# Edge-by-edge graph layers on one core: one tile of every second block by products, 0/1 matrices compared from a broadcast row, x kept in DRAM

## Chip, core and metric

One Trainium2 chip, one core. The metric is the device time of one execution in microseconds (us). A trace of one profiled execution stands beside it.

## The reference

Two graph layers over 6250 nodes with 128 features and 200000 edges, which come sorted by their destination:

```python
h = relu(layernorm(x))
z = h @ W                                  # 8 heads of 16
el, er = per-head dot products of z with attn_l, attn_r
e = leaky_relu(el[src] + er[dst], 0.2)
a = exp(e - segment_max(e, dst)[dst])
agg = segment_sum(z[src] * a, dst); out = agg / segment_sum(a, dst)
x = x + out + bias
h = relu(layernorm(x))                     # second layer
s, v = 32 scalars and 32 vectors of h, each multiplied by a weight
w0..w3 = two-step silu network of edge_attr_8, 128 weights per edge
mji = products of s[src], v[src], edge_attr_4 and w0..w3
x = x + linear(segment_sum(mji, dst) / 10)
```

Rows of a node table are thus taken by src (in any order) for each edge, and sums go to dst.

## The kernel before

The edges lie in tiles of 128, one edge to a partition; 16 tiles (KB) make a block, and there are 98 blocks (NB). Since the edges are sorted, the destinations of one block fall into a window of 128 nodes, of which 64 (WB) begin each next block. A table in DRAM holds one row of 136 floats for each node in the first layer (t0: z and el) and one of 128 in the second (t1). `gather` fetches 128 rows of a tile with one indirect DMA that POOL issues (L832), 16 for a block, into a buffer `g` (pool `fz`, five of them).

In every third block (`by_row`, from block 3) the last of the 16 tiles is fetched otherwise: SP reads 32 offsets into registers (L1063) and issues one DMA of 544 bytes for each of the 128 rows (L1067); ACT copies the finished tile `r` into `g` (`filled`, L1081). The generator `rows_by_row` spreads these issues: `rows_until` moves it on in each block, and its rows stand three blocks ahead of the block that uses them. There are three `r` buffers.

In the first layer the loop runs over blocks g. PE, DVE, ACT and SP keep the order of the program (`manual_schedule`); POOL's gathers for block g + 3 begin as a buffer comes free. In an iteration three blocks are in work: the logits and running maxima of g (`logits` L1163, `maxima`), the softmax weights, weighting and sums of g - 1 (`neighbours`, `weights`, `weighted`, `sums` L1221), and for g + 1 the destination's er. That last needs the 0/1 matrix of a tile the other way round: DVE compares the edges-by-nodes matrix `s` (`ends_of`, `one_hot` L1086, for g + 2), PE turns each by a transpose into `p_d` (`turned`, L1138), ACT casts four of them to bf16 `d` (L1140), and PE multiplies them with the three bf16 parts of er (`er_of`, L1149). Every odd block completes 128 nodes, which in the iteration after next run through `node_x`, `node_d`, `node_h`, `node_t`, `node_s` to become rows of t1; SP stores them (`node_out`, L1281) in the iteration after that. x stays in SBUF as `fx_all` through both layers.

The second layer has a loop of its own over the same blocks, with the same gathers and rows from t1.

Of the kernel before, what the change touches and what calls it, by code (L numbers as in the profile page):

```python
# [741 lines left out]
def tile_even_edges(  # L742
# [87 lines left out]
    def gather(to, table, tiles, width):  # L830
        for k, t in enumerate(tiles):
            nc.gpsimd.indirect_dma_start(  # L832
                out=to[:, k, :width], out_offset=None, in_=table,
                in_offset=bass.IndirectOffsetOnAxis(ap=src_col[:, t : t + 1], axis=0))
        return to
# [128 lines left out]
def even_edges(tc, v):  # L964
# [7 lines left out]
    with ExitStack() as ctx:  # L972
        const = ctx.enter_context(tc.tile_pool(name="fconst", bufs=1))
        z_pool = ctx.enter_context(tc.tile_pool(name="fz", bufs=5))

        def gathered(table, tiles, width):
# [7 lines left out]
        nc.sync.dma_start(rsel, v["rsel"])  # L984
        x_all = const.tile([P, NX, P], F32, name="fx_all")
        bias_b = const.tile([P, F], F32, name="fbias_b")
# [6 lines left out]
        nc.sync.dma_start(a2p, v["a2p"])  # L993
        a3p = const.tile([P, 2, P], F32, name="fa3p")
        nc.sync.dma_start(a3p, v["a3p"])
        b1 = const.tile([P, 1], F32, name="fb1")
        nc.sync.dma_start(b1, v["b1"])
        b2 = const.tile([P, 1], F32, name="fb2")
        nc.sync.dma_start(b2, v["b2"])
        wout = const.tile([P, 2, P], F32, name="fwout")  # L1000
        nc.sync.dma_start(wout, v["wout"])
        dloc = const.tile([P, NB * KB], F32, name="fdloc")
# [10 lines left out]
        with tc.tile_pool(name="fbuild", bufs=1) as build:  # L1013
# [9 lines left out]
            nc.sync.dma_start(off, nums[:, :TU])  # L1023
            nc.vector.tensor_sub(dloc[:, :TU], d_c, off)


# [17 lines left out]
        at = [const.tile([P, P], I32, name=f"fat{i}") for i in range(2)]  # L1044
        with tc.tile_pool(name="fat_ps", bufs=1, space=PSUM) as at_ps:
            col = const.tile([P, P], F32, name="fcol")
            n = NB - 1
            nc.vector.tensor_copy(col[:, :n], v["src_col"][:, KB - 1 : n * KB : KB])
            p_c = at_ps.tile([P, P], F32, name="p_c")
            nc.tensor.transpose(p_c[:n], col[:, :n], ident)  # L1050
            for i, w in enumerate((ZW, P)):
                nc.vector.tensor_scalar(at[i][:n], p_c[:n], float(4 * w), None, op0=OP.mult)
# [38 lines left out]
        def finish(b, p_u, width, carry, agg, pool):  # L1091
# [6 lines left out]
            else:  # L1098
# [4 lines left out]


        in_order = {mybir.EngineType.PE, mybir.EngineType.DVE, mybir.EngineType.Activation,
                    mybir.EngineType.SP}
        with tc.manual_schedule(engines=in_order), \
                tc.tile_pool(name="l0", bufs=2) as l0, \
                tc.tile_pool(name="l0n", bufs=2) as l0n, \
                tc.tile_pool(name="l0_ps", bufs=1, space=PSUM) as l0_ps:  # L1110

            p_n = l0_ps.tile([P, 512], F32, name="p_n")
            er_p, iota_p = p_n[:, P : 2 * P].rearrange("p (t h) -> p t h", h=H), p_n[:, 3 * P :]
            nc.scalar.copy(iota_p, iota)


# [5 lines left out]
            def masks_of(c):  # L1124
# [6 lines left out]
                nc.scalar.copy(mk[:kr], p_m[:kr, :MC])  # L1131

            def turned(c, q):
                if 4 * q < c["kt"]:
                    m = min(4, c["kt"] - 4 * q)
                    p_d = l0_ps.tile([P, 4, P], F32, name="p_d", bufs=2)
                    for k in range(m):
                        nc.tensor.transpose(p_d[:, k, :], c["s"][q][:, k, :], ident)  # L1138
                    d = c["d", q] = l0.tile([P, 4, P], BF, name="d", bufs=4)
                    nc.scalar.copy(d[:, :m], p_d[:, :m])  # L1140

# [16 lines left out]
            def logits(c, bank="pe"):  # L1158
                kt = c["kt"]
                kr = kt * H  # L1160
                e_s = l0.tile([P, KB, H], F32, name="e_s")
                pe = c["pe"] = p_n if bank == "p_n" else l0_ps.tile([P, 512], F32, name=bank, bufs=2)
                nc.vector.tensor_add(e_s[:, :kt], c["z"][:, :kt, F:], c["er"][:, :kt])  # L1163
# [59 lines left out]


            def node_rows(i, n):
                nc.sync.dma_start(x_all[:, i : i + n, :],
                                  xp[i * P : (i + n) * P].rearrange("(j p) f -> p j f", p=P))

            def with_bias(i, n):
                x_i = x_all[:, i : i + n, :]  # L1230
                nc.vector.tensor_add(x_i, x_i, bias_b[:, None, :].to_broadcast([P, n, F]))

            def node_x(u):
                i, n, agg = u["i"], u["n"], u["agg"]
                x_i = x_all[:, i : i + n, :]
                if n == 1:
# [13 lines left out]
            def node_h(u):  # L1250
                i, n = u["i"], u["n"]
                rs, mr = normal(l0n, u["mv"], u["rs"], n, f"n{n}")
                xn = u["xn"] = l0n.tile([P, 2, P], F32, name="xn")
                nc.scalar.activation(xn[:, 0, :], x_all[:, i, :], AF.Identity, bias=mr[:, 0, :],
                                     scale=rs[:, 0, :])
                if n == 2:
                    nc.vector.tensor_scalar(xn[:, 1, :], x_all[:, i + 1, :], u["mv"][:, 1, 0:1],
                                            rs[:, 1, :], op0=OP.subtract, op1=OP.mult)

            def node_t(u):  # L1260
                n = u["n"]
                u["p_n"] = p_n.rearrange("p (j f) -> p j f", f=P)
                for j in range(n):
                    nc.tensor.transpose(u["p_n"][:, j, :], u["xn"][:, j, :], ident)
                h_t = u["h_t"] = l0n.tile([P, 2, P], F32, name="h_t")
                nc.scalar.activation(h_t[:, :n], u["p_n"][:, :n], AF.Relu)

# [7 lines left out]
            def node_out(u):  # L1275
                i, n, sv = u["i"], u["n"], u["sv"]
                first = i * P - W0
                if i == 0:
                    nc.sync.dma_start(t1[: P - W0, :], sv[W0:, 0, :])
                else:  # L1280
                    nc.sync.dma_start(t1[first : first + n * P].rearrange("(j p) f -> p j f", p=P),  # L1281
                                      sv[:, :n])

            groups = [(b, 0, KB) for b in range(NB - 1)]
# [11 lines left out]
            def take_rows(g):  # L1296
                if 0 < g < NG:
                    c = cs[g]
                    t = c["b"] * KB + c["o"]
                    c["z"] = gathered(t0, range(t, t + c["kt"] - (c["b"] in by_row)), ZW)  # L1300

# [27 lines left out]
            for g in range(1, 3):  # L1329
                take_rows(g)  # L1330
            masks_of(cs[0])
            for q in range(4):
# [13 lines left out]
            for g in range(NG - 3):  # L1346
# [11 lines left out]
                nodes = []  # L1358
                logits(c)
                ends_of(n2, 0)  # L1360
                if n1 is not none:
                    masks_of(n1)
                turned(n1, 0)
                maxima(c)
                ends_of(n2, 1)
                if b4:
# [3 lines left out]
                turned(n1, 1)  # L1370
                er_of(n1, 0)
                if b4:
                    weights(b4)
                for n in nodes:
                    node_x(n)
                er_of(n1, 1)
                turned(n1, 2)
                if b4:
                    bank_of(b4)
                    weighted(b4, 0)  # L1380
                turned(n1, 3)
                er_of(n1, 2)
                if b4:
                    weighted(b4, 8)
                for n in nodes:
                    node_d(n)
# [3 lines left out]
                if b4:  # L1390
                    sums(b4, 0)
                for n in nodes:
                    node_t(n)
# [6 lines left out]
                if b4:  # L1400
                    sums(b4, 8)
                if g == NG - 4:
                    for q in range(4):
# [63 lines left out]
        with tc.manual_schedule(engines=in_order), \  # L1467
                tc.tile_pool(name="l1", bufs=3) as l1, \
                tc.tile_pool(name="l1n", bufs=2) as l1n, \
                tc.tile_pool(name="l1_ps", bufs=2, space=PSUM) as l1_ps:  # L1470

            def edge_rows(b):
# [71 lines left out]
            def sums1(u):  # L1544
# [3 lines left out]
                for k in range(m):  # L1548
                    nc.tensor.matmul(blk[b]["p_u"][:, :MW], u["s"][:, k, :], u["mj"][:, k, :],  # L1549
                                     start=k0 + k == 0, stop=k0 + k == KT[b] - 1)  # L1550

            def node1(i, agg):
                x_i = x_all[:, i, :]
                p_n = l1_ps.tile([P, 4, P], F32, name="p_n", bufs=1)
# [9 lines left out]
            def node_out1(i):  # L1564
                x_i = x_all[:, i, :]
                if i == 0:
                    nc.sync.dma_start(out[: P - W0, :], x_all[W0:, 0, :])
                else:
# [16 lines left out]

            rows, rows_until.n, late = rows_by_row(1, t1, P), 0, []
            for b in range(2):
# [9 lines left out]
            for i, u in enumerate(us):  # L1597
                b, k0, m = u["b"], u["k0"], u["m"]
                if k0 == 0:
                    take_rows(b + 2)  # L1600
                    filled(1, b, blk[b]["z"], P)
                    edge_rows(b + 2)
                if k0 == 4:
                    while late:
# [36 lines left out]
            for j in range(2):  # L1641
                for q in range(2):
                    nc.tensor.matmul(p_o[:, j, :], m_t[:, 2 * j + q, :], wout[:, q, :],
                                     start=q == 0, stop=q == 1)
            x_i = x_all[:, NX - 2 :, :]
            nc.vector.scalar_tensor_tensor(x_i, p_o[:, :2], POST, x_i, op0=OP.mult, op1=OP.add)
# [139 lines left out]
```

## Time and profile before

| | us |
|---|---|
| median of three runs (6300.1 to 6317.29) | 6316.72 |
| the profiled execution | 6201.12 |
| its span | 6199.2 |
| busy: PE / weight loads / DVE / ACT / POOL | 2970.3 / 2462.3 / 2207.9 / 1390.7 / 2919.2 |
| first layer: first and last start of L1163 in the trace | 178.6 to 2976.8 |

An engine's busy time is summed over the span; a group's line gives line, engine, operation, operands, count, then its busy time and mean ns, then the idle time just before its instructions and what ended most of it. DMA issues are not counted as busy. In the timeline a line gives the start, the length, the engine and the number of merged instructions.

### The profile page before, as it was taken

To read this page: it belongs to the slowest core of one execution; us is meant where nothing else is said; L and a number is where in the kernel's file an instruction comes from. 1 tells how busy PE (TensorE), PEld (TensorE's weight loads), DVE (VectorE), ACT (ScalarE), POOL (GpSimd) and SP (SyncE) were. 2 spreads that over 40 slices of the span, in tenths; PEclk is the share of its full clock that TensorE was granted. 3 is DMA by queue.
4 is the path that set the end of the run, shared out by engine and by line. 5 is a ranking of instruction groups with operands and counts; after the bars stand their busy time and mean duration, and the time that the engine had idled before them with its cause. 6 is when DMAs were issued, how large, how long until landed. Compare 5 with 4: busy or idle time off the path is not lost. (4 is left out here: it accounts for less than half of the span.)

```text
span 6199.2 us, 62249 instructions
## 1 busy us (share of the span) xinstructions
PE 2970.3 (48%) x14593; PEld 2462.3 (40%) x14593; DVE 2207.9 (36%) x5379; ACT 1390.7 (22%) x3612; POOL 2919.2 (47%) x3096
## 2 busy tenths in 40 slices
PE   2444434334443434444445555555555555555557
PEld 1333333333333333433334444444444444444445
DVE  3332323223232322232234334443344434443346
ACT  2212112112121212122112222222222222222223
POOL 6354454544445444454534444444444444444442
PEclk6666666656666665665677777777777777777778
DMA  5111111111111111111111111111111111111110
GB/s 133 31 41 39 39 41 40 40 41 39 39 40 42 40 39 40 39 41 39 39 30 35 38 38 37 37 37 37 38 37 36 35 39 38 36 36 37 39 38 25
DMA packets 188124, 249.35 MB, mean 40 GB/s; under 512 B 77888, under 2 KB 137952, under 8 KB 187744
## 3 DMA queue, kind: packets, MB, share of 16 engines
q0 software_dynamic: 98048, 207.27, 14.1%
q1 hardware_dynamic: 89408, 37.92, 2.4%
q8 instruction: 118, 1.93, 0.1%
q14 instruction: 262, 2.15, 0.1%
q10 hardware_dynamic: 288, 0.07, 0.0%
HBM read 234.73 MB, written 9.99 MB: 39 GB/s over the span
## 5 line engine op out<-in xcount | busy, mean ns | idle before, releaser
L832 POOL DMA_INDIRECT g<-ft,fsrc x3048 | 2885.4, 947 | 3174.9 <-issue 1510.7
L1549 PE MATMUL p_u<-mj,s 128*128 128x256 f32 x3126 | 925.2, 448 | 719.5 <-DVE mj L1541 601.3
L1549 PEld LDWEIGHTS p_u<-mj,s 128*128 128x128 f32 x3126 | 679.9, 225 | 905.1 <-DVE mj L1541 656.2
L1221 PE MATMUL p_u<-g,s 128*128 128x136 f32 x3062 | 621.5, 382 | 42.5 <-issue 39.6
L1221 PEld LDWEIGHTS p_u<-g,s 128*128 128x128 f32 x3062 | 588.6, 285 | 48.9 <-issue 44.9
L1534 DVE TENSOR_TENSOR p_w<-g,p_w 128x128 f32<-128x128 f32 x391 | 114.7, 293 | 1278.6 <-ACT p_w L1516 1099.6
L1516 ACT ACTIVATE p_w<-p_w,yb 128x64 f32<-128x64 f32 x1563 | 451.1, 289 | 475.1 <-remote 250.9
L1149 PEld LDWEIGHTS <-d 128*128 128x128 bf16 x1563 | 99.2, 113 | 845.1 <-ACT d L1140 512.0
L1512 PE MATMUL p_w<-fa3p,h 128*128 128x256 f32 x1564 | 427.4, 398 | 0.0
L1140 ACT CAST d<-p_d 128x512 bf16<-128x512 f32 x391 | 228.1, 587 | 881.3 <-remote 746.2
L1502 ACT ACTIVATE h<-p_h,fb 128x512 f32<-128x512 f32 x196 | 134.9, 688 | 1167.9 <-remote 841.8
L1512 PEld LDWEIGHTS p_w<-fa3p,h 128*128 128x128 f32 x1564 | 306.3, 206 | 142.3 <-issue 103.1
L1560 PE MATMUL p_n<-fwout,m_t 128*128 128x128 f32 x192 | 57.1, 451 | 561.6 <-ACT m_t L1558 561.6
L1138 PE MATMUL p_d<-fident,s 128*128 128x128 f32 x1563 | 320.1, 357 | 5.2 <-issue 5.2
L1216 DVE TENSOR_TENSOR g<-g,pe 128x1024 f32<-128x1024 f32 x193 | 226.2, 1213 | 226.2 <-ACT g L1207 155.4
L1499 PE MATMUL p_h<-h,fa2p 128*128 128x512 f32 x392 | 245.9, 714 | 125.2 <-ACT h L1497 98.7
L1532 DVE TENSOR_TENSOR vy<-g,p_i 128x384 f32<-128x384 f32 x391 | 215.0, 550 | 218.0 <-ACT p_i L1491 216.3
L1497 ACT ACTIVATE h<-p_h,fb 128x512 f32<-128x512 f32 x196 | 134.6, 687 | 698.2 <-PE p_h L1495 391.4
L1155 DVE TENSOR_REDUCE p_n<-p_er 128x128 f32<-128x384 f32 (+1 forms) x97 | 54.7, 563 | 663.6 <-remote 257.3
L1149 PE MATMUL p_er<-fer,d 128*128 128x24 bf16 x784 | 55.3, 185 | 467.7 <-ACT d L1140 285.2
L1086 DVE TENSOR_TENSOR s<-p_i,fdloc 128x512 f32<-128x512 f32 x391 | 269.0, 688 | 14.0 <-ACT h L1497 14.0
L1138 PEld LDWEIGHTS p_d<-fident,s 128*128 128x128 f32 x1563 | 258.2, 192 | 39.3 <-issue 30.6
(185 smaller groups left out, 3478.5 us busy)
## 6 DMA issues: line engine op xcount, KB each, us to landing
r<-ft SPq DMA_DIRECT2D x3968, 0.5 KB
r<-ft SPq DMA_DIRECT2D x3968, 0.5 KB
g<-ft,fsrc POOLq DMA_INDIRECT x3048
ft<-in_e_f_dram SPq DMA_DIRECT2D x98, 64.0 KB
yb<-in_e_y_dram SPq DMA_DIRECT2D x98, 32.0 KB
fx_all<-in_e_xp_dram SPq DMA_DIRECT2D x48, 64.0 KB
ft<-sv SPq DMA_DIRECT2D x47, 64.0 KB
out_dram<-fx_all SPq DMA_DIRECT2D x47, 64.0 KB
```

The lines of the kernel that those rows point to most:

```text
L832: nc.gpsimd.indirect_dma_start(out=to[:, k, :width], out_offset=None, in_=table, in_offset=bass.IndirectOffsetOnAxis(ap=src_col[:, t : t + ...
L1086: nc.vector.tensor_tensor(s[:, :m], iota[:, None, :].to_broadcast([P, m, P]), dloc[:, t : t + m].unsqueeze(2).to_broadcast([P, m, P]), OP. ...
L1138: nc.tensor.transpose(p_d[:, k, :], c["s"][q][:, k, :], ident)
L1140: nc.scalar.copy(d[:, :m], p_d[:, :m])
L1149: nc.tensor.matmul(c["p_er"][:, 4 * q + k].rearrange("p s h -> p (s h)"), c["d", q][:, k, :], er_w, start=True, stop=True)
L1216: nc.vector.tensor_mul(zh, zh, p_a[:, k0 : k0 + m].unsqueeze(3).to_broadcast([P, m, H, D]))
L1221: nc.tensor.matmul(c["p_u"][:, :ZW], c["s"][k // 4][:, k % 4, :], c["z"][:, k, :], start=c["o"] + k == 0, stop=c["o"] + k == KT[c["b"]] - 1)
L1499: nc.tensor.matmul(p_h.rearrange("p q e -> p (q e)"), a2p, c["h1"].rearrange("p q e -> p (q e)"), start=True, stop=True)
L1512: nc.tensor.matmul(w[:, k : k + n].rearrange("p k a u -> p (k a u)"), c["h2"][q // 4][:, q % 4, :], a3p[:, :n].rearrange("p k f -> p (k f) ...
L1516: nc.scalar.activation(w[:, k, ::2, :], w[:, k, ::2, :], AF.Copy, scale=c["yb"][:, k0 + k, 0:1])
L1532: nc.vector.tensor_mul(vy, v_n, y_p)
L1549: nc.tensor.matmul(blk[b]["p_u"][:, :MW], u["s"][:, k, :], u["mj"][:, k, :], start=k0 + k == 0, stop=k0 + k == KT[b] - 1)
```

## The change

Four things change in the first layer, and x moves for both.

- In the odd blocks from 7 to 93 (`dense`, 44 blocks) the tile before the last (KD = 14) is not gathered. The table t0 is first held in SBUF as three bf16 parts of 50 x 136 (`split`, seven times at the end of each of the first iterations). `spread` puts the sources of the tile along a row on all partitions, `ends_to` compares them with node numbers into 17 one-hot matrices, `rows_of` multiplies each with three strided slices of the three parts (51 products of up to 408 columns into one PSUM bank, six groups over two iterations), and `taken` picks one of three results for each edge.
- `turned` no longer transposes and casts. The destinations, less the window's first node, are written to DRAM once (`ends`); for each block ACT issues a DMA that broadcasts 4 KB of them to all partitions (`ends_row`), and DVE compares them with the partition's number.
- `fx_all` goes. x is loaded per 128 nodes, stored to DRAM (`x1`) after the first layer, and loaded again in the second.
- `a3p` and `wout` are loaded at the start of the second layer.

```diff
@@ gather
-        for k, t in enumerate(tiles):
+        for t in tiles:
+            k = (t - tiles[0]) % KB
@@ setup
+        x1 = dram.tile([NX, P, P], F32, name="fx1")
+        ends = dram.tile([TG, P, P], BF, name="fends_d")
-        x_all = const.tile([P, NX, P], F32, name="fx_all")
+            nc.vector.tensor_sub(d_b, d_i, off_t.unsqueeze(2).to_broadcast([P, TG, P]))
+            nc.sync.dma_start(ends.rearrange("g t e -> t g e"), d_b)
@@ first layer
+        NR = -(-NX // 3)
+        KD = KB - 2
+        dense = {b for b in range(6, NB - 4) if b % 2}
...
+            t0s = l0d.tile([P, 3, NX, ZW], BF, name="t0s")
+            def split(i, n):
+                zr = l0.tile([P, 2, ZW], F32, name="zr")[:, :n]
...
+                    nc.sync.dma_start(zr, rest.rearrange("(j p) f -> p j f", p=P))
+                r = l0.tile([P, 2, ZW], F32, name="zr2")[:, :n]
+                nc.scalar.copy(t0s[:, 0, i : i + n, :], zr)
+                nc.vector.tensor_sub(r, zr, t0s[:, 0, i : i + n, :])
+                nc.scalar.copy(t0s[:, 1, i : i + n, :], r)
+                nc.vector.tensor_sub(t0s[:, 2, i : i + n, :], r, t0s[:, 1, i : i + n, :])
+            def spread(c):
+                b = c["b"]
+                nc.tensor.matmul(at_p, key[:, b : b + 1].to_broadcast([P, P]), ident,
+                                 start=True, stop=True)
+            def ends_to(c, h):
+                n = half if h == 0 else NR - half
+                oh = c["oh", h] = ohs[:, h * half : (h + 1) * half, :]
+                nc.vector.tensor_tensor(
+                    oh[:, :n], at_p.unsqueeze(1).to_broadcast([P, n, P]),
+                    place[:, h * half : h * half + n].unsqueeze(2).to_broadcast([P, n, P]), OP.is_equal)
+            def rows_of(c, k0, n):
...
+                for k in range(k0, min(k0 + n, NR)):
+                    i = order[k]
+                    m = len(range(i, NX, NR))
+                    for s in range(3):
+                        nc.tensor.matmul(c["p_x"][:, :m, :], c["oh", k // half][:, k % half, :],
+                                         t0s[:, s, i::NR, :], start=k == 0 and s == 0,
+                                         stop=k == NR - 1 and s == 2)
+            def taken(c):
+                b, z = c["b"], c["z"][:, KD, :]
+                nc.vector.tensor_scalar(z, c["p_x"][:, 0, :], part[:, b, 0:1], None, op0=OP.mult)
+                for r in (1, 2):
+                    nc.vector.scalar_tensor_tensor(z, c["p_x"][:, r, :], part[:, b, r : r + 1], z,
+                                                   op0=OP.mult, op1=OP.add)
+            def ends_row(b):
+                if b < NB:
+                    to = ends_row.tiles[b] = l0.tile([P, KB, P], BF, name="er_d", bufs=2)
+                    g, j = divmod(b, P // KB)
+                    nc.scalar.dma_start(to, ends[g : g + 1, j * KB : (j + 1) * KB, :].to_broadcast([P, KB, P]))
             def turned(c, q):
                 if 4 * q < c["kt"]:
                     m = min(4, c["kt"] - 4 * q)
-                    p_d = l0_ps.tile([P, 4, P], F32, name="p_d", bufs=2)
-                    for k in range(m):
-                        nc.tensor.transpose(p_d[:, k, :], c["s"][q][:, k, :], ident)
-                    d = c["d", q] = l0.tile([P, 4, P], BF, name="d", bufs=4)
-                    nc.scalar.copy(d[:, :m], p_d[:, :m])
+                    d = c["d", q] = l0.tile([P, 4, P], BF, name="d")
+                    k0 = c["o"] + 4 * q
+                    nc.vector.tensor_tensor(d[:, :m], ends_row.tiles[c["b"]][:, k0 : k0 + m],
+                                            node_p.unsqueeze(2).to_broadcast([P, m, P]), OP.is_equal)
@@ node_rows, node_out
+                x_i = x_of[i] = l0n.tile([P, n, P], F32, name=f"x{n}", bufs=5 if n == 1 else 1)
+                nc.sync.dma_start(x1[i : i + n].rearrange("j p f -> p j f"), x_of.pop(i))
@@ take_rows
-                    c["z"] = gathered(t0, range(t, t + c["kt"] - (c["b"] in by_row)), ZW)
+                    c["z"] = gathered(t0, [k for k in range(t, t + c["kt"])
+                                           if not (c["b"] in by_row and k % KB == KB - 1)
+                                           and not (c["b"] in dense and k % KB == KD)], ZW)
@@ the loop over g (n1 is block g + 1, n2 block g + 2)
                 logits(c)
+                ends_row(g + 2)
+                to, was = n2["b"] in dense, n1["b"] in dense
+                if to:
+                    spread(n2)
                 ends_of(n2, 0)
...
                 maxima(c)
+                if to:
+                    ends_to(n2, 0)
+                if was:
+                    rows_of(n1, half, 4)
...
                 er_of(n1, 0)
+                if was:
+                    rows_of(n1, half + 4, NR)
                 if b4:
                     weights(b4)
+                if was:
+                    taken(n1)
...
+                if to:
+                    ends_to(n2, 1)
                 turned(n1, 3)
...
+                if to:
+                    rows_of(n2, 0, 3)
...
+                if to:
+                    rows_of(n2, 3, 3)
...
+                if to:
+                    rows_of(n2, 6, half - 6)
+                for i in range(g * 14, min(g * 14 + 14, NX), 2):
+                    split(i, min(2, NX - i))
@@ second layer
+            def node_rows1(i, n=1):
+                x_i = x_of[i] = l1n.tile([P, n, P], F32, name=f"x{n}", bufs=4 if n == 1 else 1)
+                nc.sync.dma_start(x_i, x1[i : i + n].rearrange("j p f -> p j f"))
```

## The prediction

> **What bounds the kernel now.** I read the page first, groups and DMA issues, to see which engine is near its limit in the first layer:
>
> ```profile
> L832 POOL DMA_INDIRECT g<-ft,fsrc x3048 | 2885.4, 947 | 3174.9 <-issue 1510.7
> ...
> L1140 ACT CAST d<-p_d 128x512 bf16<-128x512 f32 x391 | 228.1, 587 | 881.3 <-remote 746.2
> ...
> L1138 PE MATMUL p_d<-fident,s 128*128 128x128 f32 x1563 | 320.1, 357 | 5.2 <-issue 5.2
> ...
> r<-ft SPq DMA_DIRECT2D x3968, 0.5 KB
> ```
>
> Gathers look like the bound, but POOL is busy only 47%. So I asked who waits for whom in 500 to 2840 us, the steady part of the first layer (POOL's answer first, then ACT's; columns: total us, times, longest):
>
> ```profile
> POOL g L832 <- PE p_d L1138: 390.2, 25, 19.1
> ...
> ACT d L1140 <- remote: 598.5, 107, 13.1
> ...
> ACT g L1081 <- issue: 201.5, 13, 26.5
> ACT g L1081 <- DMA r<-ft: 159.5, 13, 22.2
> ```
>
> POOL waits for a free gather buffer, so it is ahead. ACT waits 361 us in 26 row blocks (13.9 us each) for the tile that SP fetches row by row: **SP's row stream is the bound.** Starts of the e_s addition (L1163) give 89.7 us per three blocks, and SP issues one tile of 128 rows in that time with no pause. SP's timeline, cut into 4 us windows from the start of a burst of 16 gathers at 1496.2 (1.25 us apart, over at 1516), and then between two bursts, shows what sets its pace:
>
> ```profile
> 1495.98 3.02 SPq L1067 DMA_DIRECT2D r<-ft  x9
> ...
> 1500.42 4.27 SPq L1067 DMA_DIRECT2D r<-ft  x6
> ...
> 1503.99 2.84 SPq L1067 DMA_DIRECT2D r<-ft  x3
> ...
> 1508.22 4.25 SPq L1067 DMA_DIRECT2D r<-ft  x4
> ...
> 1511.76 3.51 SPq L1067 DMA_DIRECT2D r<-ft  x2
> ...
> 1540.12 12.73 SPq L1067 DMA_DIRECT2D r<-ft  x27
> ```
>
> Nine rows in the first 4 us, two in the last; 0.47 us a row when no gather runs. Counted over 500 to 2840: 8.9, 5.3, 3.6, 2.4 and 2.0 rows in the five 4 us parts of a burst (22 in all), 0.51 us a row outside (register loads included). Two bursts of 16 and one of 15 carry 66 rows, the other 62 take 32 us: 58.8 + 32 = 90.5 us, the measured 89.7. ACT's CASTs also wait mostly in bursts; why a burst delays all is not in the trace.
>
> **What the Trainium skill says.** "DMA: Bandwidth & Descriptors", Issuing engines are not separate DMA queues: DMAs of SP, ACT and POOL share 16 engines. The trace agrees that rows suffer from gathers, at a DMA share of only 0.18. The same page, Anatomy of one DMA, prices a transfer at 2.0 us + bytes/436e3: 3.2 us as an estimate for the new 512 KB broadcast; the trace has none. "TensorE: Matmul & The Clock Gate", Back-to-back issue gap: N/1.2 ns cold, N/2.4 + 2.5 warm, so 340 and 173 ns for 408 columns; the granted clock here is 0.61. "VectorE: DVE Perf Modes", The perf-mode tier table: a tensor_tensor with a PSUM operand runs at 1x; L1086 (PSUM, 512 elements) takes 688 ns, L1216 (PSUM, 1024) 1213.
>
> **The change, part by part.**
> 1. *Gathers.* 44 blocks lose one: 44 x 1.25 = 55 us of POOL, which is not the bound. A burst's last 1.25 us carries 0.63 rows, which take 0.32 us outside: SP gains 0.93 x 44 = **-41 us**. Bound: 0 to -55.
> 2. *SP's own new issues.* 49 stores of x, at the 0.38 to 0.42 us of today's 64 KB issues: **+21 us**; 26 loads for the split are in step 6.
> 3. *PE.* 51 products of 408 columns per dense block, 0.28 us at the granted clock (0.17 to 0.41, the latter from L1128's 385 columns): 14 us (9 to 21), half in each of two iterations. 16 transposes go (8 in 1.5 to 2.0 us): -3.4 us an iteration. Net +3.7.
> 4. *DVE and ACT.* Four compares replace four CASTs: +4 x 0.69 on DVE, -4 x 0.59 on ACT; one-hots for the products add 2.6 us and the row choice about 0.9 in a dense block. Gone is the PE-ACT-PE turn, which in bursts cost some 8 to 10 us an iteration (the 598 us of CAST waits among it). Iteration of the chain: quiet, 13.8 us before (the last blocks, no gathers), I take 15 (13 to 20); in a burst 26 to 27.7 before, I take 22 (20 to 30).
> 5. *A new wait.* The broadcast row of block g+2 is issued by ACT in iteration g. The built program's instruction order, with its semaphores, shows that SP's and ACT's DMAs take eight semaphores in rotation, each waiting for the landing of the one eight before. So now SP's row stream waits for ACT's broadcasts: counting rows of the tile after the row block, row 7, 17 and 71 wait for the broadcasts of iterations 6m, 6m+1, 6m+2; row 7, 32 and 39 for those of 6m+3, +4, +5. ACT of 6m+2 waits for row 59. Behind SP's wait stand all further rows, and ACT, DVE and PE at the next row block. Before, SP ran freely. Landing: 4 us quiet, 8 late in a burst. After an odd iteration (node work) ACT is through at its end; after an even one earlier: its last copy (L1207) came 6.7 us into an iteration of 26, but a broadcast also needs DVE past the fourth compare, so I choose 0.6 of the iteration. Worked by hand with the pitches above and 15/22 us, the time from one row block to the next, in us:
>    - 6m: row 7 at 4; row 17 ready at 9, held to 9 + 4 = 13; 21 rows at 15; burst to 35: 43 rows; 47 at 37; next burst: row 59 at 43 (ACT held to 44), 69 rows at 57; iteration ends 66: 87 rows; burst to 85: 108; 20 x 0.51 = 10, landing 2: **97**.
>    - 6m+3: row 32 ready at 16.5, held to 15 + 4 = 19; row 39 ready at 24, held to 15 + 13 + 8 = 36; 41 rows at 37; burst to 57: 63; 67 at 59; burst to 78: 88; 40 x 0.51 = 20, landing 2: **100**.
>
>    197 for six blocks against 179.4: +17.6, times 13.5 (blocks 12 to 93): **+238 us**. The same with 13/20 us: 193, +184; with 20/30: 213, +454.
> 6. *Start.* Seven splits end each of iterations 0 to 3: SP load, ACT, DVE, ACT, DVE, with two buffers. ACT and DVE must wait for SP's loads, which stand behind the rows issued three blocks ahead (171 rows before the first), and SP for the buffers: 25 splits at about 2.3 us (landing plus four short operations over two buffers) = 58 us on SP, and iterations 4 to 12 then pass in lock-step. **+85 us** (40 to 130).
> 7. *The rest.* Building the lists, the store of the ends: +5. Second layer: 49 reloads of x at 0.4 us, two blocks ahead of need; SP is not its bound (ACT waits 7 us for rows in 3400 to 5900): +5. The loads of a3p and wout, now at the start of the second layer, cost nothing: its first gather waits 45.6 us there for the last store of the first (POOL's waits); uncovered, they would be 4 us.
>
> Sum: -41 + 21 + 238 + 85 + 10 = **+313** (about +180 to +590 with both ends), against the profiled execution's 6201.1 us. The median 6316.7 is 1.9% above it; I add to the median: 6630, rounded down to **6620**, as step 3 may overlap.
>
> **Rivals.**
> - *Harder lock-step (0.12).* Late in a burst a broadcast lands as the rows do there, 8 in flight at 2.0 us = 16 us, and products lengthen the iteration to 30: +34 to +45 per six blocks, about **6900 to 7000**. For it: the late-burst pace. Against: half of the broadcasts are issued near a burst's start.
> - *Lock-step does not bind, POOL's relief wins (0.14).* If without the PE-ACT-PE turn an iteration stays under 13 us in bursts as well, the broadcasts land before rows 17 and 39 come up, nothing is held, rows see shorter bursts, and 598 us of waits over 78 blocks are no longer there. Then -41 to -88 (44 x the 1.99 us per gather of the whole span), +21 and about 0 at the start: **6250 to 6300**. It decides once holds stay under 0.7 us per three blocks. Against: 14 us of products per dense block stand on the in-order PE.
> - *Gains and holds cancel (0.04)*: 6317, within 19.
> - *The products don't take the tile's place*: the gather list skips it in the source; no chance given.
>
> **How the numbers follow.** Lock-step as priced has 0.70, centre 6620, own range 6480 to 6900 from the ends above. With the rivals the range is 6300 to 6900: it leaves out most of the faster case and the worst lock-step. A measurement tells about 0.3% (19 us) from no change. Faster 0.14, same 0.04, slower 0.82.
>
> **What would show it.** Right: in the profile after, SP's queue waits for the broadcast DMA or stands in pauses at rows 17, 39 of a tile, POOL idles more, three blocks take 97 to 100 us between row copies; iterations 0 to 3 end near 400 us where block 9 stood. Step 3: products 0.28 us apart. Wrong: the row copies come every 88 us or less, or SP never pauses; or the second layer moves by more than 20 us.

## The result, and the profile after

The changed kernel takes 6574.05 us (median of four runs, 6569.71 to 6580.38), the kernel before on the same chip 6317.01 us: a ratio of **1.0411 [1.0388, 1.0434]**, slower by 257 us. 6620 was forecast.

The two pages are of different occasions. The page of before is of an execution of 6201.12 us, less than all four times of that kernel here (6300.1 to 6325.9); that of after is of one of the executions timed here, 6580.38 us. So the pages are 379 us apart where the change costs 257, and one to two per cent between them is not the change: the second layer, which only x's reloads and the loads of `a3p` and `wout` touch, takes 3183.4 us in one and 3232.3 us in the other (+1.5%, from the start of L1532 or L1667 to the end). The experiments ran on three further occasions, on chips numbered 7, 2 and 1, on which the kernel before took 6195, 3919 and 3917 us; every ratio below is against the kernel before on the same occasion. There is no page of the kernel before at 6195 us; the runs of that occasion are read beside the page at 6201 us.

Groups and DMA issues of the page after (columns as in the page of before):

```profile
L833 POOL DMA_INDIRECT g<-ft,fsrc x3004 | 2838.6, 945 | 3596.9 <-issue 1311.3
...
L1199 PE MATMUL p_x<-t0s,fz_first 128*128 128x408 bf16 (+1 forms) x2244 | 518.8, 384 | 112.9 <-issue 112.8
...
L1239 DVE TENSOR_TENSOR d<-er_d,p_i 128x512 bf16<-128x512 bf16 x391 | 264.5, 677 | 70.0 <-remote 64.8
...
L1263 DVE TENSOR_TENSOR e_s<-g,p_i 128x128 f32<-128x128 f32 x96 | 26.9, 281 | 607.6 <-ACT g L1086 516.4
...
er_d<-fends_d ACTq DMA_DIRECT2D x98, 512.0 KB
```

44 gathers fewer, the 391 CASTs and 1563 turning transposes gone, 2244 products and 391 compares come. POOL's idle time before a gather is 3596.9 us where it was 3174.9: POOL was relieved and waits longer. The e_s addition (L1263, L1163 before), the start of an iteration's chain, waits 516 us for ACT's copy of the row-fetched tile; before it was 221.9.

The waits of SP's queue over the whole span say where the rows stood (total us, times, longest):

```profile
SPq L1072 <- DMA er_d<-fends_d: 473.1, 47, 25.3
SPq L1384 <- ACT sv L1376: 78.4, 3, 33.2
SPq L1708 <- DVE x L1700: 70.0, 3, 31.3
```

SP's row issues (L1072) wait 473 us, in 47 waits, for ACT's broadcast, a transfer that they do not use. In the kernel before SP's rows (L1067) waited for nothing but other rows and the setup at the beginning; the same view of it has

```profile
SPq L1281 <- ACT sv L1273: 92.3, 3, 35.0
...
SPq L1067 <- DMA r<-ft: 63.0, 120, 1.4
```

One of the holds in the page of after stands in SP's timeline, in the stretches 1485 to 1499.5 and 1499.5 to 1522 us:

```profile
1485.30 3.33 SPq L1072 DMA_DIRECT2D r<-ft  x7
...
1512.02 8.72 SPq L1072 DMA_DIRECT2D r<-ft  x22
```

and ACT's timeline of the same time:

```profile
1505.49 0.27 ACT L1307 COPY g<-pe 128x128 f32<-128x128 f32 x1 [12.62 <-remote]
1508.29 0.33 ACTq L1230 DMA_DIRECT2D er_d<-fends_d  x1
1514.73 0.48 ACT L1223 COPY mk<-p_m 128x385 f32<-128x385 f32 x1 [8.97 <-PE p_m L1220]
```

SP stops at 1488.6, after row 38 of its tile. ACT stands in order behind its copies of a slow iteration (12.6 us in one wait) and issues the broadcast only at 1508.3; 3.7 us later SP goes on with row 39. In the trace the semaphore for which row 39 waits is the one that this broadcast signals, and so it is in all 36 pauses over 2.9 us at rows 17, 32 and 39 from block 15's tile on. Over these tiles the mean time from one row to the next, by the row's place in its tile, exceeds 4 us in three places only: row 17 (9.5 us, in every other tile), and in the tiles between row 32 (4.4) and row 39 (21.8). These are rows that the semaphore order named. Not all of row 32's time is a hold: at rows 0, 32, 64 and 96 SP loads offsets into registers, and row 32 takes 2.6 us in the kernel before. Row 64's 4.0 is near before's 3.7.

POOL's and ACT's waits in 500 to 2840 us:

```profile
POOL g L833 <- issue: 527.1, 1022, 9.6
POOL g L833 <- PE p_m L1220: 390.1, 20, 27.8
POOL g L833 <- PE p_x L1199: 186.0, 12, 27.7
```

```profile
ACT g L1086 <- DMA r<-ft: 339.4, 20, 41.4
ACT g L1307 <- remote: 279.3, 28, 12.9
```

So there is a circle: ACT waits for rows (17 us a time, 41 at most) and SP waits for ACT's broadcast; that POOL waits for gather buffers behind both is a reading of the PE operations named.

Six blocks, from the starts of the e_s addition (blocks 12 to 90), take **198.9 us**, before 180.0. Start to start, from block 12 on, by the iteration's place in a round of six (6m is block 12 and every sixth after it; 6m and +3 begin with a row-fetched tile):

| us | 6m | +1 | +2 | +3 | +4 | +5 | sum |
|---|---|---|---|---|---|---|---|
| before | 19.6 | 31.1 | 39.9 | 21.2 | 26.6 | 41.6 | 180.0 |
| after | 15.5 | 28.2 | 47.3 | 19.0 | 29.9 | 58.9 | 198.8 |

Every third iteration (+2 and +5), at whose end ACT stands until the next row-fetched tile is there, is longer by 7.4 and 17.3 us; the two ahead of it together are 7.0 us shorter (6m, +1) and 1.1 longer (+3, +4). Block 12 begins at 561.5 us of the profile's time, before at 481.1.

### The profile page after: what moved, and what is told of

Its sections match the earlier page's. It is cut to its first block, busy times and chain, and to the rows that moved or that the text cites. A ratio compares the mean times of both kernels' runs of the same rounds, so it can differ in the third digit from the quotient of the medians.

```text
span 6578.6 us, 64273 instructions
## 1 busy us (share of the span) xinstructions
PE 3148.7 (48%) x15362; PEld 2429.3 (37%) x15362; DVE 2609.3 (40%) x6066; ACT 1187.8 (18%) x3272; POOL 2872.2 (44%) x3052
## 5 line engine op out<-in xcount | busy, mean ns | idle before, releaser
L833 POOL DMA_INDIRECT g<-ft,fsrc x3004 | 2838.6, 945 | 3596.9 <-issue 1311.3
L1091 DVE TENSOR_TENSOR s<-p_i,fdloc 128x512 f32<-128x512 f32 x782 | 536.1, 686 | 138.4 <-PE p_i L1175 94.4
L1321 PE MATMUL p_u<-g,s 128*128 128x136 f32 x3062 | 578.7, 367 | 3.7 <-issue 3.3
L1199 PE MATMUL p_x<-t0s,fz_first 128*128 128x408 bf16 (+1 forms) x2244 | 518.8, 384 | 112.9 <-issue 112.8
L1321 PEld LDWEIGHTS p_u<-g,s 128*128 128x128 f32 x3062 | 556.6, 273 | 3.8 <-issue 3.3
L1266 PE MATMUL pe<-fident,e_s 128*128 128x128 f32 x98 | 32.6, 332 | 683.1 <-DVE e_s L1264 571.1
L1199 PEld LDWEIGHTS <-fz_first 128*128 128x128 bf16 x2244 | 240.9, 110 | 275.6 <-issue 163.9
L1667 DVE TENSOR_TENSOR vy<-g,p_i 128x384 f32<-128x384 f32 x391 | 214.7, 549 | 201.2 <-ACT p_i L1626 199.7
L1239 DVE TENSOR_TENSOR d<-er_d,p_i 128x512 bf16<-128x512 bf16 x391 | 264.5, 677 | 70.0 <-remote 64.8
L1266 PEld LDWEIGHTS pe<-fident,e_s 128*128 128x128 f32 x98 | 15.1, 154 | 694.1 <-issue 562.6
L1263 DVE TENSOR_TENSOR e_s<-g,p_i 128x128 f32<-128x128 f32 x96 | 26.9, 281 | 607.6 <-ACT g L1086 516.4
```

What stands on the lines that cost most here:

```text
L833: nc.gpsimd.indirect_dma_start(out=to[:, k, :width], out_offset=None, in_=table, in_offset=bass.IndirectOffsetOnAxis(ap=src_col[:, t : t + ...
L1091: nc.vector.tensor_tensor(s[:, :m], iota[:, None, :].to_broadcast([P, m, P]), dloc[:, t : t + m].unsqueeze(2).to_broadcast([P, m, P]), OP. ...
L1199: nc.tensor.matmul(c["p_x"][:, :m, :], c["oh", k // half][:, k % half, :], t0s[:, s, i::NR, :], start=k == 0 and s == 0, stop=k == NR - 1 ...
L1239: nc.vector.tensor_tensor(d[:, :m], ends_row.tiles[c["b"]][:, k0 : k0 + m], node_p.unsqueeze(2).to_broadcast([P, m, P]), OP.is_equal)
L1321: nc.tensor.matmul(c["p_u"][:, :ZW], c["s"][k // 4][:, k % 4, :], c["z"][:, k, :], start=c["o"] + k == 0, stop=c["o"] + k == KT[c["b"]] - 1)
L1667: nc.vector.tensor_mul(vy, v_n, y_p)
```

## Experiments

The theory: SP's rows and ACT's broadcasts take their completion semaphores in one rotation, so SP is held until ACT, in order behind its work, has issued and landed a broadcast; that makes the steady part slower, and the splits make the start slower. Rivals: the products on PE make the iteration longer; POOL or the whole iteration chain, not SP, sets the pace.

**The broadcast on POOL's queue.** One word moved:

```diff
-                    nc.scalar.dma_start(to, ends[g : g + 1, ...
+                    nc.gpsimd.dma_start(to, ends[g : g + 1, ...
```

> The changed kernel with the 512 KB broadcast of the destinations issued on POOL's queue instead of ACT's; nothing else differs. Its semaphores then rotate with the gathers', and no row of SP's stream waits for it. Lock-step theory: the holds of SP at rows 17, 32 and 39 (35 us per six blocks in the profile after) go, six blocks fall from 198.9 to about 180, and the time from 6574 to about 6320 (6290 to 6400; 98 more issues lengthen POOL's bursts). Rival, the cost lies in the added work and traffic (519 us of products, 50 MB of broadcasts): six blocks stay above 195 and the time stays at 6540 to 6600.

Measured: 6251.43 us against 6195.01, **1.0082 [1.0052, 1.0113]**: most of the 4.1% is gone. SP no longer waits for the broadcast at all; the first entries among its waits are

```profile
SPq L1708 <- DVE x L1700: 106.4, 19, 31.3
SPq L1384 <- ACT sv L1376: 83.3, 3, 30.3
...
SPq L1072 <- DMA r<-ft: 46.4, 90, 1.4
```

and rows 17, 32 and 39 stand no longer than in the kernel before. Six blocks take 179.1 us, as before. What is left stands at the start: block 12 begins at 549.3 us, 68 later than in the page of before, more than the whole 56 us. The products run here as in the changed kernel, so their PE time (518.8 us in the page of after) by itself does not make six blocks longer. Nor shorter: the six classes of iteration are nearly even now (26.4 to 33.0 us), ACT waits for rows for 40 us only (339 in the changed kernel), and ACT's waits in 500 to 2840 us are inside the chain:

```profile
ACT g L1307 <- remote: 425.5, 38, 14.4
ACT mk L1223 <- PE p_m L1220: 422.0, 52, 10.8
ACT h_t L1369 <- remote: 323.6, 32, 11.2
```

So with the hold removed SP is no longer the bound. That the iteration chain gives nearly the same 179 us by itself is not shown, because the move adds a wait of its own: in 500 to 2840 us POOL stands ahead of its broadcasts until DVE's compares give their buffer free, and no gather passes it.

```profile
POOL er_d L1230 <- DVE d L1239: 266.2, 40, 8.6
```

What the kernel would take with neither wait was not measured.

**No products** (the tile is gathered again, no splits):

```diff
-        dense = {b for b in range(6, NB - 4) if b % 2}
+        dense = set()
...
-                for i in range(g * 14, min(g * 14 + 14, NX), 2):
-                    split(i, min(2, NX - i))
```

> The changed kernel without dense blocks: all their tiles are gathered, no split of the table, no products; the compared 0/1 matrices with ACT's broadcast and x in DRAM stay. Lock-step theory: SP is still held at rows 14, 32 and 39; shorter iterations (13 us quiet, 20 in a burst) give 193 us per six blocks, no start cost: 6500 (6440 to 6580). Rival, the products on PE are what costs: 6317 within 30 or below.

Measured: 6333.61 against 6195.01, **1.0217 [1.0187, 1.0248]**, +139 us. Six blocks 188.3, block 12 at 511.1. SP's wait remains, shorter:

```profile
SPq L1072 <- DMA er_d<-fends_d: 154.9, 31, 8.7
```

With none of the products rows are still held (14: 7.9 us, 32: 5.5, 39: 8.0), and this kernel has more than half of the loss; the compares and x in DRAM are in it too, and no run at this pace has these without ACT's broadcasts. Row 39's 8.0 us against 21.8 show one thing that the products add: later broadcasts. The six classes say where they come from: 6m and +3 take 12.4 and 12.5 us here, +1 and +4 take 14.1 and 14.7 with 9 gathers in each, and the waiting for rows stands in +2 and +5 (68.1 and 66.4). With the products +1 and +4 take 28.2 and 29.9, with 16 and 14 gathers in them.

**No splits** (the table's parts are zero, so the rows of the product tiles are left out; the products run):

```diff
             t0s = l0d.tile([P, 3, NX, ZW], BF, name="t0s")
+            nc.gpsimd.memset(t0s, 0.0)
...
-                for i in range(g * 14, min(g * 14 + 14, NX), 2):
-                    split(i, min(2, NX - i))
```

> The changed kernel without the 25 splits of the table in iterations 0 to 3: the three parts are zeros, so the products give zeros and that tile's rows are left out of the sums; every instruction of the later iterations stands. Start theory (the splits tie the first iterations to SP's late loads): the twelfth block is reached near 490 us instead of 572 and the time falls by 80 (50 to 110), to 6495; six blocks stay at 199. Rival, the start is bound by something else (the lists, the store of the ends): no more than 20 us come back.

Measured: 6398.75 against 6195.01, **1.0329 [1.0298, 1.0361]**. Block 12 begins at 518.4 us instead of 561.5 (the expectation counts from a zero 10.5 us earlier, its 572 is the same block), so the splits cost some 43 us of the start by the traces, which are of two occasions; by the ratios, 0.8% or 51 us. 80 had been expected (50 to 110). Rows 17, 32 and 39 are held as with the splits (9.2, 4.4, 20.0 us); six blocks take 192.5, where 199 had been expected.

**The kernel before with a small DMA on ACT.** In each iteration of the first layer ACT issues one DMA of 256 bytes whose data nobody reads:

```diff
+                small = l0.tile([1, P], BF, name="small", bufs=2)
+                nc.scalar.dma_start(small, v["rsel"][0:1, 0, :])
```

> The kernel before with one added DMA of 256 bytes in each iteration of the first layer, issued by ACT where the changed kernel issues its broadcast; nobody reads it. In the order of the built program rows 6, 11 and 71, or 7, 33 and 39, of a tile then wait for it. Lock-step theory: the semaphores alone cost as much as the change, six blocks 179 to 210 (iterations are longer here, 21 and 27 us), the time 6317 to 6700 (6550 to 6800). Rival, traffic or added work costs: 98 issues of 0.1 us on ACT, the time 6317 to 6340.

Measured: 6284.49 against 6195.01 on the same occasion, **1.0153 [1.0117, 1.0189]**, +89 us; six blocks 184.1. SP waits for these 256 bytes, at rows 11 and 39 of its tiles (5.1 and 7.8 us):

```profile
SPq L1067 <- DMA small<-in_e_rsel_dram: 101.7, 24, 11.8
```

The direction is the theory's, the size is not: 240 to 480 had been expected. So neither the 512 KB nor the compare is needed to hold SP: it is enough that ACT has a DMA in the rotation. ACT's own 96 issues take 0.23 us each, 22 us together, and can't be the whole +89. And 101.7 us of holds cost 89, which agrees with the prediction's view that SP's stream is on the path of the kernel before in this condition. One to one is no rule: in the changed kernel 473 us of holds stand beside a loss of 257.

**The change again, and the kernel before, on the quick occasions.** On the next occasion, on chip 2, the kernel before takes 3919.32 us, 38% less than 6317, with the same program.

> The changed kernel unaltered, on the chip of the runs beside it, so that its trace and theirs are of one chip. Lock-step theory: 1.041 times the kernel before here too; six blocks near 195, holds at rows 17, 32 and 39; the second layer within 20 us of 3183. If the 49 us that the second layer grew by in the first trace are the change's (reloads of x), it stays at 3230.

Measured: 4210.45 against 3919.32, **1.0744 [1.0726, 1.0762]**: +291 us, near the +257 in us, 1.8 times as much in per cent. SP's waits there:

```profile
SPq L1072 <- DMA er_d<-fends_d: 422.0, 84, 12.1
```

> The kernel before, unchanged, for a profile on the same occasion as its neighbours. Both theories: the ratio is 1.000 within 0.003. If this occasion is one in which the kernel takes about 6200 to 6300 us, its six blocks take 180 us and rows slow within a burst of gathers (over 1 us a row at its end); if it is the quick one (about 3900 us), six blocks take 117 to 120 us, gathers stand 1.25 us apart without a pause, and rows keep their pace in bursts.

Measured: 3916.32 against 3916.68, 1.000. POOL's waits in this profile of the kernel before, and one line of SP's timeline:

```profile
POOL g L832 <- issue: 865.9, 2839, 0.3
POOL g L832 <- DMA ft<-sv: 28.9, 1, 28.9
```

```profile
1007.08 34.44 SPq L1067 DMA_DIRECT2D r<-ft  x84
```

No gather waits over 0.3 us within a layer: gathers stand 1.25 us apart without a pause, and rows keep 0.41 us through it. The bound of the kernel before is **POOL** here, not SP: 94 gathers in six blocks (96 less two row-fetched tiles) by 1.25 make 117.5 us, and 117.4 is measured.

Both quick profiles together split the loss at one pace (they are of two chips, on which the kernel before takes the same time within 0.1%). Block 12: 304.9 to 397.9, +93. Blocks 12 to 93: 1584.4 to 1802.8, **+218** (six blocks 117.4 to 133.9, with 8.8, 8.8 and 10.7 us at rows 17, 32 and 39). End of the first layer: -19. Second layer: 1917.8 to 1915.6, -2. Together +291 before rounding, as measured.

**Every fourth block by rows, in the kernel before** (a test of SP as the bound: a quarter fewer rows to issue, 7 more gathers):

```diff
-        by_row = [b for b in range(3, NB - 2) if b % 3 == 0]
+        every = {0: 4, 1: 3}
+        rows_in = {k: [b for b in range(3, NB - 2) if (b - 3) % n == 0] for k, n in every.items()}
```

> The kernel before with row-fetched tiles in every fourth block instead of every third in the first layer (the second layer keeps thirds): 24 tiles of SP's rows instead of 31, 7 more gathers on POOL. SP theory: four blocks take 78.8 us of bursts with 87 rows in them and 41 rows at 0.51 us, 100 us, so six blocks fall from 180 to 150 to 165 (the chain of PE, ACT and DVE needs 26 us in a burst), the time by 200 to 350. Rival, POOL's gathers or the chain set the pace: no change, or up to 30 us slower.

Measured, beside 3919.32: 3926.39, 1.0018 [1.0011, 1.0025]. The expected gain did not come; the rival held. Six blocks have 94.5 gathers, 118.1 us at 1.25, and take 118.1. This is no test of SP at 6200 us, as it ran where POOL is the bound.

**The broadcast on POOL without products, and that with every fourth block:**

> The changed kernel with the broadcast on POOL's queue and without dense blocks (no split, no products): the compared matrices and x in DRAM alone, without the holds. Lock-step theory: SP's rows bound it again as in the kernel before, six blocks 179 to 182, the time within 30 us of the kernel before. Rival, the compares on DVE or the broadcasts' traffic cost in themselves: 60 us or more above it.

> The kernel e8 with row-fetched tiles in every fourth block of the first layer. SP theory: with SP relieved and an iteration of 13 to 20 us, POOL's 16 gathers and a broadcast (21 us) or SP's 25 us a block set the pace: six blocks 150 (135 to 165), the time 300 to 400 below the kernel before. Rival, bursts without a pause lengthen the iteration to 28 us and more, as in e1: six blocks 165 to 180, under 150 us gained.

Measured, beside 3919.32: 4021.33 (1.0259 [1.0242, 1.0276]) and 4032.6 (1.0289 [1.0271, 1.0306]). Both missed. Six blocks of the first take 121.2 us: 94 gathers by 1.25 make 117.5, and the 3.7 us left are 0.62 for each of six broadcasts. The group of these issues in that run is near it, with a mean of 0.58:

```profile
L1230 POOL DMA_DIRECT2D er_d<-fends_d x98 | 57.1, 583 | 24.1 <-DVE d L1239 23.9
```

These broadcasts make up half of the +102 over the layer. The rest is the start: the first e_s addition begins at 163.9 us instead of 94.9, and block 12 at 356.7 instead of 304.9. POOL's first broadcast stands behind all gathers that find a free buffer, and is issued at 151 us, where ACT issues it at 84 in the changed kernel.

**The small DMA on POOL's queue, in the kernel before.** As above, with `nc.gpsimd` for `nc.scalar`.

> The kernel before with one added DMA of 256 bytes per iteration of the first layer, as in the run with ACT's small DMA, but issued by POOL. Lock-step theory: the loss comes from SP's rows and ACT's DMAs sharing semaphores in rotation, and POOL's DMAs take no part in it: SP never waits for the small DMA, ratio within 0.003 of 1 where POOL is not the bound (kernel before near 6200 us), and 98 more issues of about 1 us, up to 1.02, where POOL's gathers are (near 3900 us). Rival, an added DMA costs the rows by its landing or its ring whichever engine issues it: 1.012 to 1.019 as with ACT, with holds in SP's rows.

Measured: 4016.15 against 3916.68, **1.0253 [1.0239, 1.0267]**, +99 us, but in another way than expected. POOL keeps no hand-written order, and issued the 96 DMAs of the trace between 143 and 343 us, in runs with bursts of gathers between them; one stretch of POOL's timeline:

```profile
231.64 0.96 POOL L1361 DMA_DIRECT2D small<-in_e_rsel_dram  x2 [1.03 <-DMA small<-in_e_rsel_dram]
233.88 0.96 POOL L1361 DMA_DIRECT2D small<-in_e_rsel_dram  x2 [1.28 <-DMA small<-in_e_rsel_dram]
```

Two buffers, some 2 us a pair, and no gather within such a stretch: block 12 begins 98 us late, and six blocks take 117.4 us as before. SP waits for none of them, which agrees with the theory, but they were over before the steady part, so the run doesn't separate the rival there. The kernels with the broadcast on POOL do: it is issued through the whole layer, and no row is held.

**Two steps at the start.** The broadcast on POOL, with the splits spread thin,

```diff
-        dense = {b for b in range(6, NB - 4) if b % 2}
+        dense = {b for b in range(17, NB - 4) if b % 2}
...
-                for i in range(g * 14, min(g * 14 + 14, NX), 2):
+                for i in range(g * 4, min(g * 4 + 4, NX), 2):
```

> The kernel after with the broadcast issued by POOL, and with the splits spread over 13 iterations (4 tiles of the table in each, not 14); the products then begin at block 17, so 39 blocks have them and not 44. Theory: the start was a queue of splits on SP and ACT in four iterations and passes in lock-step; spread thin it hides under the gathers: block 12 begins 40 to 60 us earlier than with the broadcast on POOL alone, which makes 0.999 to 1.003 on an occasion near 6200 us. Rival: the splits' loads wait behind SP's rows wherever they stand, and every one holds ACT and DVE for it: no gain against the broadcast on POOL alone, 1.008 or more.

and the broadcast on POOL without splits (edit as above):

> The kernel after with the broadcast issued by POOL, and without the splits: the table's three parts are zero, so the rows of the product tiles are left out of the result; the products run as before. Theory: the start is worth 43 to 68 us, so 0.998 to 1.003 on an occasion near 6200 us, and the steady part stays where the broadcast on POOL alone had it (179 us for six blocks). Rival: the rest of the loss against the kernel before stands in the steady part, and the time stays at 1.006 or more.

Measured against 3916.68: 3976.16, **1.0154 [1.014, 1.0168]**, and 3949.63, **1.0085 [1.0071, 1.0099]**. Six blocks take 117.2 and 117.4 us. Here the products do save what they should: 91 gathers by 1.25 and six broadcasts by 0.6 make 117.4. The three gathers saved and the six issues added cancel, and the products themselves stay hidden. Beside the changed kernel's 133.9 us on a quick occasion this is the clearest test of the hold: with the broadcast on POOL's queue all of the steady part's loss is gone. What is left is the start, block 12 at 368.2 and 339.4 us against 304.9: +63 with thin splits, +34 with none. Both were expected for a chip near 6200 us, so whether thin splits recover the start there was not seen; no run in that condition has the broadcast on POOL and the splits spread. No version beats the kernel before.

## Why the prediction was right, step by step

The mechanism held: the wait for ACT's broadcasts, which no line of the diff names, was read out of the built program's order of semaphores, and the holds stand at the rows named. Without it (the broadcast on POOL) 1.041 becomes 1.008 at the slow pace, and on the quick occasions six blocks return from 133.9 us to the 117.4 of the kernel before. +257 us were measured where the steps gave +313. The steps:

1. *Gathers, -41.* Not seen as a gain. With the holds gone six blocks take 179.1 us at the slow pace (180.0 before) although three gathers are missing. On the quick occasion the gathers are worth 3 x 1.25 us and the broadcasts on POOL eat them.
2. *SP's stores of x, +21.* In the trace after at 0.38 us each (L1386), as priced; their effect was not measured by itself.
3. *Products.* 518.8 us over 2244 are 0.23 us each, between the prediction's 0.17 and 0.34; 0.28 was taken: 11.8 us a dense block, not 14. The mean 384 ns in the page is a pipelined matmul's length, not its pitch.
4. *Iterations.* The compare takes 677 ns (0.69 taken from a row with a PSUM operand; "VectorE: DVE Perf Modes", The perf-mode tier table, says that such an operation runs at 1x; the trace agrees in that bf16 inputs bring nothing beside the 688 ns of L1086, but no run has the compare without a PSUM operand). Quiet iterations take 15.5 and 19.0 us (15 taken). **In a burst an iteration takes 28 to 30 us, 22 were taken**: this is the term that was mis-sized. Before, the same two take 31.1 and 26.6 us by the table, 28.9 in the mean, where the prediction read 26 to 27.7. The gone PE-ACT-PE turn was credited with 4 to 6 us that the changed kernel does not show. But without the products these iterations take 14.1 and 14.7 us, with 9 gathers in them, and the quiet ones 12.4: so the turn's going did seem to pay, and what takes it back comes with the products and the fuller bursts. That is more than their PE time of 5.9 us an iteration; which wait it is stays open (ACT's copies of L1307 and L1369 wait 279 and 172 us for what the profile doesn't name).
5. *The new wait.* Landing was taken as 4 us quiet, 8 in a burst. From ACT's issue to the held row the trace has 3.8 us in the median at all three rows (3.3 to 5.0), in bursts too. "DMA: Bandwidth & Descriptors", Anatomy of one DMA, whose price is for DMAs issued by POOL, gave 3.2 as an estimate; for ACT's broadcast the trace has 0.6 more, and the measurement decides. The two errors point in opposite ways: the longer iteration made ACT's broadcast later (row 39 held 21.8 us, 12 in the hand-worked schedule), the shorter landing gave some back, and 198.9 us for six blocks are near the 197 forecast. That the sum fits is thus partly luck. Part of it is the occasion too: reduced by the second layer's 1.5%, six blocks take 196. And the 198.9 hold what steps 1 and 2 count for themselves, 2.8 us of gain and 1.3 of cost by the prediction's prices, so that 195.5 is the forecast to compare. The row copies, though, are not 97 and 100 us apart but 91 and 108: the hand-worked schedule had the sum, not the parts.
6. *Start, +85.* Block 12 is 80.4 us later in the pages and 93.0 on the quick occasions. Leaving the splits out takes 43 to 51 us off; the splits' part had been put at 58. ACT waits 152.8 us in 14 waits for their loads, with one of 118.2, as loads that stand behind the rows would make it. The lock-step of iterations 4 to 12, the other part of the step, does not show: block 4 is already 96 us late (333.4 against 237.5 us, where the prediction had iterations 0 to 3 end near 400), and block 12 no more than 80.
7. *The rest, +10.* The second layer moves by -2 us where both kernels have a profile on the quick occasions: +5 was too much, and nothing followed from it.

Which terms make up the 56 us between +313 and +257 is not known, as no page of the kernel before is of that occasion. Two slips of the prediction's own sums change little: 58.8 + 32 is 90.8, not 90.5, and its terms' ends add up to about +200 and +615, not +180 and +590.

"SP's row stream is the bound" fits the pace of 6200 us, where 101.7 us of holds cost 89, though of the 361 us of ACT's waits that it was read from the profile names the rows for 159.5 only. It is not a property of the program: on the quick occasions POOL is the bound of the same instructions, with a share of 74% in place of 47%. The loss in us is nearly the same there; I read it as the loop of SP, ACT and the iteration chain being slower than either bound, but why the two losses are so near each other no run isolates.

Of the rivals, the harder lock-step had the right burst iteration (30 us) and the wrong landing (16 us; 3.8 measured), and so ended too high. POOL's relief came true in no run: with the holds away the kernel is still not faster than before, though POOL's own broadcasts are then in the way. Gains and holds did not cancel.

## What to carry to other kernels

A DMA added on one queue may hold another queue that does not use its data, as it did here: look in the built program for what each queue's issues wait for before costing it at its landing, and ask how late the in-order engine that issues it will be; a 256-byte transfer in each iteration cost 1.5% that way. Moving it to a queue outside the rotation removes the hold, but it then takes its place in that engine's order: 0.6 us an issue where POOL is the bound, and a late start where it stands behind gathers. Gathers taken from POOL, which idled half of the time at the slow pace, brought nothing there: before pricing such a relief, ask what makes the engine idle.

## Not expected of the hardware

The same program ran at 6195 to 6317 us on some occasions and at 3917 to 3919 on two others. The gather issue takes the same time in both (947 and 945 ns in the mean, 1.25 us apart), and busy times of DVE and ACT are the same within 1%. The packets of the largest DMA queue (q0), too, take the same time on the 16 DMA engines: 14.1% of 6199 us and 22.3% of 3917 us are both 874 us. The granted clock stands higher in the quick one (POOL, clock and q0 rows of the two pages of the kernel before, at 6201 us and then at 3917):

```profile
POOL 6354454544445444454534444444444444444442
PEclk6666666656666665665677777777777777777778
...
q0 software_dynamic: 98048, 207.27, 14.1%
```

```profile
POOL 6777777777777777777757777777777777777776
PEclk6766666666666666666679999999999999999999
...
q0 software_dynamic: 98048, 207.27, 22.3%
```

In the first layer the clock is nearly the same in both (0.62 and 0.65), so the clock does not explain a first layer that is a third shorter. What differs there is what happens between engines: in the page at 6201 us rows slow from 9 to 2 in 4 us within a burst of gathers and the other engines' waits grow with them; at 3917 us gathers run without a pause and rows keep 0.41 us. What makes one condition or the other was not found. The record numbers the chips of the three later occasions, 7 for the slow one and 2 and 1 for the quick ones; no chip was seen in both conditions, so whether it is the chip or the occasion stays open.
